# Tokens sorted by expert on TensorE and moved to the expert pages in runs by SP, in place of row scatters by GpSimd, in a fused GNN and mixture-of-experts kernel

## The chip, the core and the metric

One core of a Trainium2 chip. The metric is the device time of one execution in microseconds. The kernel before took 3548.45 us, the median of three runs (3544.21 to 3556.92).

## What is computed

A graph layer over 12,500 nodes and 212,500 weighted edges, then a mixture of eight experts, each token going to its best expert only and each expert taking at most C = 1,954 tokens, in order of the token's number. Cut to what matters:

```python
# graph layer: features of the source nodes, weighted, summed by destination
msgs = features[edge_src] * edge_weight[:, None]
agg = jax.ops.segment_sum(msgs, edge_dst, num_segments=12500)
gnn = agg @ W.T + b                                  # features = layernorm(x)
x = x + gnn
# experts: h = layernorm(x)
logits = h @ gate_w + gate_b
idx = argmax(softmax(logits))                        # one expert for each token
pos = cumsum(one_hot(idx))[token, idx] - 1           # place in that expert's list
kept = pos < C
buf[idx, pos] = h                                    # for the kept tokens
y = (relu(buf @ w1 + b1) @ w2 + b2)[idx, pos] * prob * kept
x = x + nan_to_num(y)
```

All data are float32; x has 256 columns, an expert 1,024 hidden ones. With the reference's inputs the experts get between 781 and 3,325 tokens, and no expert gets more than 46 of the 128 tokens of one tile.

## The kernel before

**Edges.** Edges come sorted by destination. They are cut in 1,661 edge tiles of 128. For each, GpSimd (POOL) gathers 128 rows of the normalized features by an indirect DMA (`gather`, L582), VectorE (DVE) builds a 128x128 matrix of edge weights by destination (`onehot`, L590), and TensorE (PE) multiplies the two (`product`, L599), summing 15 edge tiles in PSUM. ScalarE (ACT) copies such a group sum out (L602). The gathered tiles `m` have 32 buffers.

**Nodes.** A generator, `nodes`, works through 98 tiles of 128 nodes in chunks of eight tiles (the last chunks have 5, 4 and 1). For each node tile it shifts and adds the group sums (L635), multiplies with W (L644), adds x (L647). `Ffn.route` then normalizes the chunk, computes the gate and the best expert of each token, and its place in the expert's list (`pre`, `pos`), and makes rows `rt` of 260 columns: the token's 256 values, mean, inverse deviation, probability and number.

**Pages.** `buf` in HBM holds 128 pages of 128 rows, 16 for each expert, filled at the start with a value that names no token. `put` (L341) scatters the 128 rows of one node tile to their places in the pages, by an indirect DMA of POOL. Each is queued in `pool_q` and issued one per step. `listing` then finds which pages have become full, and `nodes` waits until the queue is empty before it hands these pages to the experts.

**Experts.** A second generator, `experts`, loads a page or a pair of pages (`load`, L439) and the expert's weights (1 MB each for w1 and w2) by SP, 20 steps before it uses them; `fresh` normalizes (L459), `turn` transposes, `products` multiplies (L483 and L494), `finish` scales, and `send` (L525) scatters the finished rows to the output by an indirect DMA of POOL. Chunks 0 to 9 hand over pairs, chunks 10 to 12 single pages, and after the last chunk all full pages left and each expert's last, partly filled page follow.

**The order.** One loop writes all of this out by hand. Each step of it issues one gather, then one scatter from `pool_q` or else a piece of a finished page's work, then the products of the edge tile that was gathered 16 steps earlier (`LEAD`), then one yield of `nodes` and one of `experts`. Pieces of expert work are spaced by `PACE` (3.0 steps for pairs, 2.3 for single pages). Every engine works its queue in this order. After step 1,661 there are no gathers left and the loop goes on until the pages are done.

Each DMA signals one of eight semaphores of its kind in turn: eight for the DMAs of POOL, eight that SP and ACT share. A DMA waits for the one that had its semaphore before.

**Two guards.** `rest` works off more single pages when the lists were longer than planned, and a slow path recomputes everything when `n_bad`, a count of edges out of the expected order, is not zero.

Of the kernel before, what the change touches and what calls it, by code (L numbers as in the profile page):

```python
# [9 lines left out]
F32 = mybir.dt.float32  # L10
# [8 lines left out]
P = 128  # L19
# [26 lines left out]
FILL = float(1 << 20)  # L46


SLOTS = [(2, n) for n in (0, 3, 4, 4, 4, 4, 4, 4, 4, 2)] + [(1, n) for n in (10, 4, 3)]
# [9 lines left out]
LOADED = 20  # L59
PACE = {1: 2.3, 2: 3.0}  # L60


# [32 lines left out]
def gnn_moe_kernel(ctx: ExitStack, tc: tile.TileContext, x, src, dst, ew, wT, gb, gate_w, gate_b,  # L95
# [6 lines left out]
    feat = dram.tile([N, D], F32, name="feat")  # L102
    buf = dram.tile([(NP_ + 2) * P, RW], F32, name="buf")

    ident = consts.tile([P, P], F32, name="ident")
# [43 lines left out]
    nc.vector.tensor_scalar(need, even, float(P), float(P), op0=ALU.mult, op1=ALU.add)  # L149
    n_bad = consts.tile([1, 1], I32, name="n_bad")  # L150

    gb_sb = consts.tile([P, D], F32, name="gb_sb")
# [4 lines left out]
    keep = ctx.enter_context(tc.tile_pool(name="keep", bufs=1))  # L157
    run = keep.tile([P, E], F32, name="run")
    posted = keep.tile([P, 1], F32, name="posted")
    place_of = keep.tile([P, 1], F32, name="place_of")  # L160
# [58 lines left out]
    class Ffn:  # L219
        def __init__(self, p3, p4, ps_m, ps_t, ps_h, ps_y):  # L220
            self.p3, self.p4 = p3, p4
            self.ps_m, self.ps_t, self.ps_h, self.ps_y = ps_m, ps_t, ps_h, ps_y
            self.puts, self.sends, self.loads = [], [], []
            self.paired = False

            self.before = None
# [4 lines left out]
            nc.vector.memset(taken, 0.0)  # L231

        def fill(self):
# [11 lines left out]

        def route(self, rt, ln, t0, nt, rows):
            p3 = self.p3
# [91 lines left out]

            def put(j):  # L340
                s = nc.gpsimd.indirect_dma_start(  # L341
                    out=buf[:, :], out_offset=bass.IndirectOffsetOnAxis(ap=to[:, j, :], axis=0),
                    in_=rt[:rows, j, :], in_offset=None, bounds_check=NP_ * P - 1, oob_is_err=False)
# [6 lines left out]
                self.before = s  # L350

            self.put = [(put, j) for j in range(nt)]


# [57 lines left out]
        def last(self):  # L412
            p3 = self.p3
            c8 = p3.tile([P, E], F32, name="c8")
            nc.vector.tensor_mul(c8, run, mine)
            c = p3.tile([P, 1], F32, name="c1")
            nc.vector.tensor_reduce(c, c8, axis=AX.X, op=ALU.add)
            nc.vector.tensor_scalar(c, c, float(C), page0, op0=ALU.min, op1=ALU.subtract)
            some = p3.tile([P, 1], F32, name="some")
            nc.vector.tensor_scalar(some, c, 1.0, None, op0=ALU.is_ge)  # L420
            nc.vector.scalar_tensor_tensor(some, c, float(P), some, op0=ALU.is_lt, op1=ALU.mult)
            nc.vector.tensor_scalar(c8, mine, some, None, op0=ALU.mult)
            pi = self.psum("pi")
            nc.tensor.matmul(pi[0:1, :E], page_of[:, 0:1], c8, start=True, stop=True)
            lp = p3.tile([1, E], I32, name="lp", bufs=1)
            nc.vector.tensor_scalar(lp, pi[0:1, :E], float(NP_ * P), None, op0=ALU.add)
            return lp

        def load(self, of, li, i, e=None):
            p4 = self.p4  # L430
            at = li[0:1, 0, i:i + 1] if e is None else li[0:1, e:e + 1]
# [6 lines left out]
            pg = p4.tile([P, 2, RW], F32, name="pg", bufs=4)  # L438
            self.loads.append(nc.sync.dma_start(  # L439
                pg[:, :of, :], buf[ds(row, of * P), :].rearrange("(a p) d -> p a d", p=P)))  # L440
            return (of, pg) + self.weights(e)
# [58 lines left out]
        def finish(self, of, pg, py, b2_sb):  # L500
# [22 lines left out]

            def send(a):
                s = nc.gpsimd.indirect_dma_start(  # L525
                    out=out[:, :], out_offset=bass.IndirectOffsetOnAxis(ap=to[:, a, :], axis=0),
                    in_=z[:, a, :], in_offset=None, bounds_check=N - 1, oob_is_err=False)
                for o in self.sends:
                    if o is not self.before:
                        tc.declare_no_dep(s.ins, o.ins, reason="each token is in one page")  # L530
                self.sends.append(s)
                self.before = s

# [12 lines left out]
        def rest(self):  # L546
            left = nc.values_load(left_i, min_val=0, max_val=LEFT,  # L547
                                  skip_runtime_bounds_check_because="a count of pages")
            with tc.If(left > 0):
                self.sends, self.before = [], None  # L550
                for i in range(4):
                    self.page(1, self.li, i)
                with tc.If(left > 4):
                    self.sends = []
                    for i in range(4, LEFT):
                        self.page(1, self.li, i)


    with tc.tile_pool(name="edges", bufs=1) as edges:
# [8 lines left out]
        with tc.tile_pool(name="p2", bufs=32) as p2, tc.tile_pool(name="p2h", bufs=12) as p2h, \  # L568
# [8 lines left out]
            sums, ms, hs = {}, {}, {}  # L577
            pool_q, pages = [], []

            def gather(k):  # L580
# [3 lines left out]
                    in_offset=bass.IndirectOffsetOnAxis(ap=src_i[:, k:k + 1], axis=0))  # L584
                ffn.before = None
                ms[k] = m
# [18 lines left out]
            def nodes():  # L605
# [10 lines left out]
                for c, (t0, nt, rows) in enumerate(CHUNKS):  # L616
                    rt = p3.tile([P, CH, RW], F32, name="rt")
                    ln = ln_new(p3)
                    for t in range(t0, t0 + nt):
# [32 lines left out]
                    last = c == len(CHUNKS) - 1  # L652
                    if last or SLOTS[c][1]:
# [68 lines left out]
            def check():  # L722
# [17 lines left out]
                nc.tensor.matmul(pc, ones[:, 0:1], cnt, start=True, stop=True)  # L740
                nc.vector.tensor_scalar(n_bad, pc, -1.0, float(P * KT), op0=ALU.mult, op1=ALU.add)

# [106 lines left out]
            for f, j in pool_q:  # L849
# [4 lines left out]

    some = nc.values_load(n_bad[0:1, 0:1], min_val=0, max_val=P * KT,
                          skip_runtime_bounds_check_because="a count of edges")
    with tc.If(some > 0):
# [132 lines left out]
```

## Time and profile before

| | |
|---|---|
| median of three runs | 3548.45 us |
| the profiled execution | 2575.36 us |
| its span, first to last instruction | 2573.6 us |
| mean granted TensorE clock in it | 0.867 |
| indirect DMAs of POOL: gathers, scatters to pages, scatters to the output | 1661, 98, 91 |
| mean time of one: gather from the features, to pages, to the output | 972, 1009, 1001 ns |

The profiled execution is shorter than the runs by some 973 us; the profile shows that execution only. PE, DVE, ACT, POOL and SP are the engines' names in it, PEld is the loading of a matmul's stationary operand, and a q behind an engine's name means its queue or sequencer. In the lines of groups the number after x counts instructions; a float32 product counts as two matmul instructions. The slices show the course of the run:

```profile
PE   2467788797799698698699699698698797698797
PEld 1345545575577477477487487477476574487686
DVE  6775433444344344354453444444443443454432
ACT  5750000111012012012012012012011110122232
POOL 7647777777777777777777777777777777777111
PEclk9678666799799799799799799799799797799898
```

Each digit is the busy share in tenths of a fortieth of the span, 64 us; PEclk is the granted clock in tenths. The first three slices are the normalizing of the features, the last three come after the last gather. Between them a chunk of eight node tiles repeats about every 190 us.

### The profile page before, as it was taken

The numbers are of one execution on the slowest core, as the hardware profiler recorded it, in microseconds if no ns is written. First come the engines' busy times: TensorE is split into PE (matmuls) and PEld (weight loads), VectorE is DVE, ScalarE is ACT, GpSimd is POOL, SyncE is SP. The second block draws the span as 40 slices with busy tenths as digits, with TensorE's granted clock in tenths as the row PEclk, the third lists the DMA queues.
The fourth block names the chain that finished last, engine by engine and source line by source line (L and its number), as shares of the span: only waits on it lengthen the run. The fifth ranks groups of instructions, "written<-read, shape, count | busy, mean of one in ns | idle before, by whom it ended". The sixth has DMA issues, their size and how long they took to land. (4 is left out here: it accounts for less than half of the span.)

```text
span 2573.6 us, 30236 instructions
## 1 busy us (share of the span) xinstructions
PE 2046.4 (80%) x9082; PEld 1599.7 (62%) x9082; DVE 1177.0 (46%) x4287; ACT 504.9 (20%) x1315; POOL 1805.4 (70%) x1859
## 2 busy tenths in 40 slices
PE   2467788797799698698699699698698797698797
PEld 1345545575577477477487487477476574487686
DVE  6775433444344344354453444444443443454432
ACT  5750000111012012012012012012011110122232
POOL 7647777777777777777777777777777777777111
PEclk9678666799799799799799799799799797799898
DMA  8759434644654654654654654654654354497485
GB/s 282 252 172 368 127 109 124 193 145 122 211 166 123 219 157 122 209 165 121 204 170 122 201 175 122 204 170 123 194 177 121 110 186 122 138 309 247 153 273 176
DMA packets 264700, 455.60 MB, mean 177 GB/s; under 512 B 44799, under 2 KB 190406, under 8 KB 264520
## 3 DMA queue, kind: packets, MB, share of 16 engines
q0 software_dynamic: 88800, 240.41, 30.5%
q1 hardware_dynamic: 136210, 174.68, 21.1%
q10 hardware_dynamic: 39510, 38.41, 4.6%
q8 instruction: 77, 1.26, 0.2%
q14 instruction: 103, 0.84, 0.1%
HBM read 387.86 MB, written 67.83 MB: 177 GB/s over the span
## 5 line engine op out<-in xcount | busy, mean ns | idle before, releaser
L582 POOL DMA_INDIRECT m<-feat,src_i x1549 | 1506.2, 972 | 493.0 <-issue 222.1
L599 PE MATMUL pw<-m,h 128*128 128x256 f32 x3322 | 1114.9, 451 | 408.7 <-DMA m<-feat,src_i 297.8
L599 PEld LDWEIGHTS pw<-m,h 128*128 128x128 f32 x3322 | 654.0, 219 | 701.9 <-DMA m<-feat,src_i 406.2
L590 DVE TENSOR_SCALAR h<-cols,rel,w_sb 128x128 f32<-128x128 f32 x1549 | 467.0, 360 | 405.6 <-PE pw L599 397.3
L483 PE MATMUL ph<-gT,w_sb 128*128 128x256 f32 (+1 forms) x1856 | 362.7, 346 | 0.0
L494 PE MATMUL py<-w_sb,hT 128*128 128x256 f32 x1456 | 349.8, 385 | 0.0
L483 PEld LDWEIGHTS ph<-gT,w_sb 128*128 128x128 f32 x1856 | 308.7, 199 | 33.3
L494 PEld LDWEIGHTS py<-w_sb,hT 128*128 128x128 f32 x1456 | 274.6, 193 | 35.1
L487 ACT ACTIVATE hT<-ph,b_sb 128x256 f32<-128x256 f32 (+1 forms) x464 | 167.9, 426 | 419.4 <-PE ph L483 409.7
L525 POOL DMA_INDIRECT out<-z,tok x91 | 91.1, 1001 | 153.2 <-DVE tok L522 111.7
L635 PEld LDWEIGHTS ms<-s,ws 128*128 128x128 f32 x1116 | 177.1, 216 | 18.2 <-issue 3.7
L635 PE MATMUL ms<-s,ws 128*128 128x128 f32 x1116 | 176.3, 299 | 3.4 <-DVE s L612 3.3
L647 DVE TENSOR_TENSOR rt<-xt,ms 128x256 f32<-128x256 f32 x98 | 41.2, 420 | 287.8 <-PE ms L644 287.7
L602 ACT COPY ws<-pw 128x256 f32<-128x256 f32 x111 | 41.4, 373 | 631.6 <-PE pw L599 631.6
L582 POOL DMA_INDIRECT m<-in_x,src_i x112 | 108.1, 965 | 53.6 <-issue 20.1
L504 DVE TENSOR_TENSOR y<-py,b_sb 128x512 f32<-128x512 f32 (+1 forms) x58 | 33.4, 576 | 240.4 <-PE py L494 240.4
L341 POOL DMA_INDIRECT buf<-rt,to x98 | 98.9, 1009 | 54.0 <-issue 19.2
L459 DVE TENSOR_SCALAR xg<-pg 128x256 f32<-128x256 f32 x91 | 35.3, 418 | 174.1 <-DMA pg<-buf 174.1
L507 ACT ACTIVATE y<-y,pg 128x256 f32<-128x256 f32 x91 | 42.6, 502 | 340.4 <-DVE y L504 294.5
L644 PE MATMUL ms<-wT_sb,aT 128*128 128x256 f32 x392 | 107.4, 399 | 2.4 <-ACT aT L639 2.4
L639 ACT COPY aT<-ms 128x256 f32<-128x256 f32 x98 | 36.5, 373 | 275.6 <-PE ms L635 269.9
L644 PEld LDWEIGHTS ms<-wT_sb,aT 128*128 128x128 f32 x392 | 77.4, 199 | 15.8 <-ACT aT L639 4.4
(159 smaller groups left out, 1253.6 us busy)
## 6 DMA issues: line engine op xcount, KB each, us to landing
w_sb<-in_w SPq DMA_DIRECT2D x116, 1024.0 KB, 11.4
m<-feat,src_i POOLq DMA_INDIRECT x1549, 2.8
buf<-fill SPq DMA_DIRECT2D x13, 1300.0 KB, 18.4
xt<-in_x ACTq DMA_DIRECT2D x97, 128.0 KB, 2.4
xt<-in_x SPq DMA_DIRECT2D x12, 1024.0 KB, 8.1
feat<-xn ACTq DMA_DIRECT2D x12, 1024.0 KB, 9.7
out<-rt ACTq DMA_DIRECT2D x11, 1024.0 KB, 4.9
pg<-buf SPq DMA_DIRECT2D x33, 260.0 KB, 13.4
```

Of the source, the lines that this page charges most:

```text
L341: s = nc.gpsimd.indirect_dma_start(out=buf[:, :], out_offset=bass.IndirectOffsetOnAxis(ap=to[:, j, :], axis=0), in_=rt[:rows, j, :], in_of ...
L483: nc.tensor.matmul(ph[:, c:c + n], w1_sb[:, k, f * P:(f + 1) * P], xT[:, k * n:(k + 1) * n], start=(k == 0), stop=(k == 1))
L487: nc.scalar.activation(hT[:, f, :n], ph[:, c:c + n], AF.Relu, bias=b1_sb[:, f:f + 1])
L494: nc.tensor.matmul(py[:, a, :], hT[:, f, a * P:(a + 1) * P], w2_sb[:, f, :], start=(f == 0), stop=(f == F // P - 1))
L507: nc.scalar.activation(y[:, a, :], y[:, a, :], AF.Copy, scale=pg[:, a, D + 2:D + 3])
L525: s = nc.gpsimd.indirect_dma_start(out=out[:, :], out_offset=bass.IndirectOffsetOnAxis(ap=to[:, a, :], axis=0), in_=z[:, a, :], in_offset= ...
L582: nc.gpsimd.indirect_dma_start(out=m, out_offset=None, in_=x[:, :] if k < RAW else feat[:, :], in_offset=bass.IndirectOffsetOnAxis(ap=src_ ...
L590: nc.vector.tensor_scalar(h, cols, rel[:, k:k + 1], w_sb[:, k:k + 1] if w is None else w, op0=ALU.is_equal, op1=ALU.mult)
L599: nc.tensor.matmul(product.pw, hs.pop(k), ms.pop(k), start=(j == 0), stop=last)
L602: nc.scalar.copy(ws, product.pw)
L635: nc.tensor.matmul(pa[:, k * P:(k + 1) * P], sums[g][:, k * P:(k + 1) * P], shifts[t, g], start=(g == gs[0]), stop=(g == gs[-1]))
L644: nc.tensor.matmul(px[:rows, :], aT[:, k * P:k * P + rows], wT_sb[:, k, :], start=(k == 0), stop=(k == 1))
```

## The change

- The node tiles of chunks 0 to 10 (`SORTED = 11`, eleven chunks of eight tiles) are no longer scattered row by row. `sort` builds for each tile a 128x128 permutation from the tokens' places within the tile, ordered by expert (L590's kind of operation), multiplies `rt` with it on TensorE, copies the sorted rows back over `rt`, and stores the chunk into one of three HBM tensors, `by_expert`, from ACT's queue.
- For each tile and expert, `move` copies 64 rows (`RUN`) from the place where the expert's run begins in `by_expert` to the expert's next free row in the pages, HBM to HBM, by SP. Both row numbers are loaded into registers from SBUF, four at a time. A run is shorter than 64 rows as a rule; the rows behind it are overwritten by the expert's next run, which therefore waits for the move of the same expert before it. Two moves are issued per step of the loop (`MOVES`), from a queue of their own, and `nodes` waits until both queues are empty.
- Where an expert's last run leaves foreign rows behind the last token of a page, `fresh` adds a large number to their token number when the partly filled pages are worked off (`none`, `part`).
- If an expert has more than 64 tokens in a tile (`most`), the slow path is taken.
- Scatters of POOL (`put` of chunks 11 to 13, and `send`) no longer wait for the one before; a `nop` stands ahead of each.

```diff
+RUN = 64
+MOVES = 2
+SORTED = 11
...
+    by_expert = [dram.tile([CH * P + RUN, RW], F32, name=f"by_expert{i}") for i in range(3)]
...
         def fill(self):
...
+            for s in by_expert:
+                nc.sync.dma_start(s[CH * P:, :], fill[:RUN, :])
...
             pre = small("pre")
+            if place is not None:
+
+                runs = p3.tile([P, CH, 2, E], I32, name="runs")
+                off = p3.tile([P, CH, E], F32, name="off")
+                nc.vector.memset(off[:, :, 0:1], 0.0)
+                for e in range(E - 1):
+                    nc.vector.tensor_add(off[:, :nt, e + 1], off[:, :nt, e], pp[:, 1, :nt, e])
+                nc.vector.tensor_add(pre, pp[:rows, 0, :nt, :], off[:rows, :nt, :])
+                nc.vector.tensor_add(runs[0:1, :nt, 0, :], off[0:1, :nt, :],
+                                     tokc[0:1, :nt, None].to_broadcast([1, nt, E]))
...
             for j in range(nt):
-                nc.vector.tensor_add(pre[:, j, :], pp[:rows, 0, j, :], run[:rows, :])
+                if place is None:
+                    nc.vector.tensor_add(pre[:, j, :], pp[:rows, 0, j, :], run[:rows, :])
+                else:
+                    nc.vector.scalar_tensor_tensor(runs[0:1, j, 1, :], run[0:1, :], float(C), pages_of,
+                                                   op0=ALU.min, op1=ALU.add)
                 nc.vector.tensor_add(run, run, pp[:, 1, j, :])
...
+            if place is not None:
+                nc.vector.tensor_scalar_add(pos, pos, -1.0)
+                yield from self.sort(rt, pos, runs, place, nt, rows)
+                return
...
             def put(j):
+                nc.gpsimd.nop()
                 s = nc.gpsimd.indirect_dma_start(
...
                 for i in self.puts:
-                    if i is not self.before:
-                        tc.declare_no_dep(s.ins, i.ins, reason="each token has a row of its own")
+                    tc.declare_no_dep(s.ins, i.ins, reason="each token has a row of its own")
...
+        def sort(self, rt, pos, runs, place, nt, rows):
+            for j in range(nt):
+                r = self.p3.tile([P, P], F32, name="perm")
+                nc.vector.tensor_scalar(r[:rows, :], cols[:rows, :], pos[:, j, :], None,
+                                        op0=ALU.is_equal)
+                yield
+                ps = self.psum("ps")[:, :RW]
+                nc.tensor.matmul(ps, r[:rows, :], rt[:rows, j, :], start=True, stop=True)
+                nc.scalar.copy(rt[:, j, :], ps)
+            yield
+            nc.scalar.dma_start(place[:nt * P, :].rearrange("(j p) d -> p j d", p=P), rt[:, :nt, :])
+
+            at = {}
+
+            def move(j, e):
+
+                nc.sync.nop()
+                for i, f in ((0, e), (1, e)) if e % 4 == 0 else ():
+                    _, v = nc.values_load_multi_w_load_instructions(
+                        runs[0:1, j, i, f:f + 4], engines=[mybir.EngineType.SP], min_val=0,
+                        max_val=((E - 1) * PE_ * P + C if i else CH * P),
+                        skip_runtime_bounds_check_because="rows of the chunk, and of the pages")
+                    at.update(((i, f + a), v[a]) for a in range(4))
+                s = nc.sync.dma_start(buf[ds(at[1, e], RUN), :], place[ds(at[0, e], RUN), :])
+                for i in self.moves:
+                    if i is not self.moved[e]:
+                        tc.declare_no_dep(s.ins, i.ins, reason="another expert's, or one before that")
+                for i in self.loads:
+                    tc.declare_no_dep(s.ins, i.ins, reason="pages that are read are full")
+                self.moves.append(s)
+                self.moved[e] = s
+
+            self.put = [(move, j, e) for j in range(nt) for e in range(E)]
...
         def fresh(self, of, pg):
             xg = self.p4.tile([P, 2, D], F32, name="xg")
+            if self.part[id(pg)] is not None:
+                nc.vector.tensor_add(pg[:, 0, D + 3:RW], pg[:, 0, D + 3:RW], self.part[id(pg)])
...
             def send(a):
+                nc.gpsimd.nop()
...
-                    yield from ffn.route(rt, ln, t0, nt, rows)
-                    pool_q.extend(ffn.put)
+                    yield from ffn.route(rt, ln, t0, nt, rows,
+                                         by_expert[c % 3] if c < SORTED else None)
+                    (moves if c < SORTED else pool_q).extend(ffn.put)
...
-                        while pool_q:
+                        while moves or pool_q:
                             yield
...
                 if s < KT:
                     gather(s)
+                for f, j, e in moves[:MOVES]:
+                    f(j, e)
+                del moves[:MOVES]
                 if pool_q:
                     f, j = pool_q.pop(0)
                     f(j)
```

More of the change, by code (lines that the diff above doesn't have):

```diff
@@ L150, in gnn_moe_kernel @@
     n_bad = consts.tile([1, 1], I32, name="n_bad")
+    bad = consts.tile([1, 1], F32, name="bad")
+    pages_of = consts.tile([1, E], F32, name="pages_of")
+    nc.vector.tensor_scalar(pages_of, cols[0:1, :E], float(PE_ * P), None, op0=ALU.mult)
     gb_sb = consts.tile([P, D], F32, name="gb_sb")
@@ L158, in gnn_moe_kernel @@
     run = keep.tile([P, E], F32, name="run")
+    most = keep.tile([1, 1], F32, name="most")
     posted = keep.tile([P, 1], F32, name="posted")
@@ L223, in __init__ @@
             self.puts, self.sends, self.loads = [], [], []
+            self.part = {}
             self.paired = False
-            self.before = None
             nc.vector.memset(run, 0.0)
@@ L231, in __init__ @@
             nc.vector.memset(taken, 0.0)
+            nc.vector.memset(most, 0.0)
+            self.moved, self.moves = [None] * E, []
         def fill(self):
@@ L243, in psum, with route @@
             return self.ps_m.tile([P, 512], F32, name="ms")
-        def route(self, rt, ln, t0, nt, rows):
+        def route(self, rt, ln, t0, nt, rows, place=None):
             p3 = self.p3
@@ L319, in route @@
             pre = small("pre")
-            for j in range(nt):
-                nc.vector.tensor_add(pre[:, j, :], pp[:rows, 0, j, :], run[:rows, :])
+            if place is not None:
[7 more added lines that the diff above has]
+                                     tokc[0:1, :nt, None].to_broadcast([1, nt, E]))
+                much = p3.tile([1, 1], F32, name="much")
+                nc.vector.tensor_reduce(much, pp[0:1, 1, :nt, :], axis=AX.XY, op=ALU.max)
+                nc.vector.tensor_tensor(most, most, much, op=ALU.max)
+            for j in range(nt):
+                if place is None:
[3 more added lines that the diff above has]
+                                                   op0=ALU.min, op1=ALU.add)
                 nc.vector.tensor_add(run, run, pp[:, 1, j, :])
@@ L349, in put @@
                 self.puts.append(s)
-                self.before = s
             self.put = [(put, j) for j in range(nt)]
+        def sort(self, rt, pos, runs, place, nt, rows):
[27 more added lines that the diff above has]
+            self.put = [(move, j, e) for j in range(nt) for e in range(E)]
         def split(self):
@@ L426, in last @@
             nc.vector.tensor_scalar(lp, pi[0:1, :E], float(NP_ * P), None, op0=ALU.add)
+            cs = p3.tile([P, E], F32, name="cs", bufs=1)
+            nc.vector.tensor_scalar(cs, c8, c, None, op0=ALU.mult)
+            pc = self.psum("pc")[:, :E]
+            nc.tensor.matmul(pc, ones, cs, start=True, stop=True)
+            self.none = p3.tile([P, E], F32, name="none", bufs=1)
+            nc.vector.tensor_scalar(self.none, pc, pcol, float(SKIP), op0=ALU.is_le, op1=ALU.mult)
             return lp
@@ L430, in load @@
             p4 = self.p4
+            none = None if e is None else self.none[:, e:e + 1]
             at = li[0:1, 0, i:i + 1] if e is None else li[0:1, e:e + 1]
@@ L438, in load @@
             pg = p4.tile([P, 2, RW], F32, name="pg", bufs=4)
+            self.part[id(pg)] = none
             self.loads.append(nc.sync.dma_start(
@@ L528, in send @@
                 for o in self.sends:
-                    if o is not self.before:
-                        tc.declare_no_dep(s.ins, o.ins, reason="each token is in one page")
+                    tc.declare_no_dep(s.ins, o.ins, reason="each token is in one page")
                 self.sends.append(s)
-                self.before = s
             for _ in range(3):
@@ L549, in rest @@
             with tc.If(left > 0):
-                self.sends, self.before = [], None
+                self.sends = []
                 for i in range(4):
@@ L577, in gnn_moe_kernel @@
             sums, ms, hs = {}, {}, {}
-            pool_q, pages = [], []
+            moves, pool_q, pages = [], [], []
             def gather(k):
@@ L584, in gather @@
                     in_offset=bass.IndirectOffsetOnAxis(ap=src_i[:, k:k + 1], axis=0))
-                ffn.before = None
                 ms[k] = m
@@ L649, in nodes @@
                         ln_stats(ln, x1, t - t0, rows)
-                    yield from ffn.route(rt, ln, t0, nt, rows)
-                    pool_q.extend(ffn.put)
+                    yield from ffn.route(rt, ln, t0, nt, rows,
+                                         by_expert[c % 3] if c < SORTED else None)
+                    (moves if c < SORTED else pool_q).extend(ffn.put)
                     last = c == len(CHUNKS) - 1
+                    if last:
+                        nc.vector.scalar_tensor_tensor(n_bad, most, float(RUN), bad, op0=ALU.is_gt,
+                                                       op1=ALU.add)
                     if last or SLOTS[c][1]:
@@ L740, in check @@
                 nc.tensor.matmul(pc, ones[:, 0:1], cnt, start=True, stop=True)
-                nc.vector.tensor_scalar(n_bad, pc, -1.0, float(P * KT), op0=ALU.mult, op1=ALU.add)
+                nc.vector.tensor_scalar(bad, pc, -1.0, float(P * KT), op0=ALU.mult, op1=ALU.add)
             B = CH + RB
@@ L851, in gnn_moe_kernel @@
             ffn.rest()
-    some = nc.values_load(n_bad[0:1, 0:1], min_val=0, max_val=P * KT,
-                          skip_runtime_bounds_check_because="a count of edges")
+    some = nc.values_load(n_bad[0:1, 0:1], min_val=0, max_val=P * KT + 1,
+                          skip_runtime_bounds_check_because="a count of edges, and one")
     with tc.If(some > 0):
```

## The prediction

> **What bounds the kernel now.** I read the engines' totals and slices first, then the table of stretches, then the groups, then Pool's order of time.
>
> ```profile
> span 2573.6 us, 30236 instructions
> PE 2046.4 (80%) x9082; PEld 1599.7 (62%) x9082; DVE 1177.0 (46%) x4287; ACT 504.9 (20%) x1315; POOL 1805.4 (70%) x1859
> ```
>
> PE is the busiest by share, Pool second. The stretches turn this round:
>
> ```profile
> 1400.00:1600.00 200.00, 169.05 (x770) 136.94 (x768) 88.69 (x313) 33.43 (x78) 152.26 (x157) 0.90 0.53 164
> 1600.00:1800.00 200.00, 165.92 (x765) 132.55 (x765) 90.61 (x316) 33.75 (x77) 152.20 (x157) 0.93 0.53 163
> ...
> 2400.00:2500.00 100.00, 82.84 (x508) 75.01 (x507) 40.49 (x178) 33.60 (x101) 13.63 (x14) 0.88 0.66 209
> ```
>
> Columns: stretch, length, busy us of PE, PEld, DVE, ACT, POOL (instructions), granted TensorE clock, DMA share, GB/s. From 400 to 2200 us Pool issues 155 to 159 operations in every 200 us, whatever PE does. That is a rate limit; its two parts stand in Pool's timeline:
>
> ```profile
> 2217.69 0.94 POOL L582 DMA_INDIRECT m<-feat,src_i  x1 [0.30 <-PE ms L635]
> 2218.93 1.00 POOL L341 DMA_INDIRECT buf<-rt,to  x1 [0.30 <-issue]
> 2220.24 0.98 POOL L582 DMA_INDIRECT m<-feat,src_i  x1 [0.30 <-PE ms L635]
> 2221.53 1.02 POOL L341 DMA_INDIRECT buf<-rt,to  x1 [0.30 <-issue]
> ```
>
> The bracket is always 0.30 us, whoever is named as releaser: it is the sequencer's own gap. A gather costs 1.25 us, a scatter to the pages (L341) 1.31. PE's waits point the same way:
>
> ```profile
> L599 PE MATMUL pw<-m,h 128*128 128x256 f32 x3322 | 1114.9, 451 | 408.7 <-DMA m<-feat,src_i 297.8
> ...
> L341 POOL DMA_INDIRECT buf<-rt,to x98 | 98.9, 1009 | 54.0 <-issue 19.2
> ```
>
> PE waits for gathered rows. So Pool carries this execution until its last gather at about 2380 us; then PE works off expert pages, one per 7.59 us (2468.80 to 2476.38 here; x is the number of matmuls):
>
> ```profile
> 2468.80 3.62 PE L494 MATMUL py<-w_sb,hT 128*128 128x256 f32 x16
> 2472.25 3.73 PE L483 MATMUL ph<-gT,w_sb 128*128 128x128 f32 x32
> 2476.14 0.41 PE L468 MATMUL pT<-ident,xg 128*128 128x128 f32 x2
> 2476.38 3.62 PE L494 MATMUL py<-w_sb,hT 128*128 128x256 f32 x16
> ```
>
> One thing doesn't fit: the profiled execution took 2575.4 us (span 2573.6 and 1.8 around it), the median of the runs is 3548.45. No view names the missing 973 us. One resource of the trace has two speeds:
>
> ```profile
> 924.10:927.60 3.50, 3.50 (x9) 2.75 (x9) 0.36 (x1) 0.00 (x0) 2.59 (x4) 0.50 0.70 225
> ```
>
> ```profile
> 924.23 3.62 PE L483 MATMUL ph<-gT,w_sb 128*128 128x256 f32 x8
> ```
>
> At clock 0.50 eight 256-column matmuls take 3.62 us; at 1.00 sixteen do (above).
>
> **What the Trainium skill says.** "DMA: Bandwidth & Descriptors", section Issuing engines are not separate DMA queues: SP, ACT and Pool feed the same 16 engines, and another issuer saves only issue time. Here issue time is what binds, and the engines have room (share 0.53), so the advice is met. The same page, Two DMAs through the same engine are not ordered: only a completion semaphore orders them; hence an expert's runs, which overlap, wait for one another. No run here has such copies. The same page, Anatomy of one DMA: 2.0 us plus bytes at 436 GB/s; the old scatters land after 2.6 us, which agrees. "TensorE: Matmul & The Clock Gate", Part 1: the clock is at half or full, and work releases it; the 0.50 and 1.00 above agree.
>
> **The change part by part.**
>
> Removed: 88 of 98 scatters (chunks 0 to 10; 5 + 4 + 1 stay). Each 1.009 busy and 0.30 gap: 88 x 1.31 = 115 us of Pool, on the path. Pool's instruction order has nothing in their place, and its nops leave no instruction. Waits between scatters were 11.7 us in all for L341, nearly all after the last gather, where the chain of the last chunks runs beside waiting pages: counted at nothing.
>
> Added on PE: per tile a sort of 128x260, two matmuls at 0.22 us (clock 1.00) to 0.44 (0.50): 39 to 77 us in all. Cover: PE idles 31 to 34 us in each 200 us above, and a chunk of eight tiles needs 3.5 to 7. Nothing on the path; uncovered, it costs the whole 77.
>
> Added on DVE and ACT: 88 permutations like L590 (0.36 us) 32 us; 88 copies of a PSUM tile like L602 (0.373) 33 us; some 25 short operations per chunk at about 0.1 us, 28 us. DVE is busy 45%, ACT 17%: nothing.
>
> Added on ACT's queue: one 1 MB store per chunk, like the store of out rows already there (4.9 us to landing). It is issued after the sort, and the moves wait for it.
>
> Added on SP: 704 moves of 64 rows (66 KB, HBM to HBM) with 352 register loads. SP's issues stand 0.60 us apart and a pair of register loads adds 0.67:
>
> ```profile
> 1064.66 0.35 SPq L446 DMA_DIRECT2D b_sb<-in_b  x1
> 1065.26 0.34 SPq L448 DMA_DIRECT2D b_sb<-in_b  x1
> 1065.84 0.38 SPq L450 DMA_DIRECT2D w_sb<-in_w  x1
> 1066.45 0.38 SPq L452 DMA_DIRECT2D w_sb<-in_w  x1
> 1067.72 0.37 SPq L439 DMA_DIRECT2D pg<-buf  x1
> ```
>
> A tile is 8 x 0.60 + 2 x 0.67 = 6.1 us, a chunk 49. A move's own time is unseen. Below: 2.15 us, an estimate by the page's formula; above: 8.8 us, the median landing of a 130 KB page load behind weights. An expert's next move is eight later, so it can hold SP at 8.8 / 8 = 1.1 us a move at worst, 70 us a chunk. I take 49. Queued behind the moves on SP are the page load L439 and the weights; DVE waits for these (174 us in 21 waits already) and PE behind it. Cover: Pool may run 16 gathers (20 us) further before the 32 buffers of m stop it. The moves start about 13 steps ahead of Pool, because ACT runs that far ahead of it, and are written over 32 steps = 40 us: 49 us end within 3 us of the place where the loads stand. Nothing at 49; at 70 about the cushion.
>
> Moved: counting the yields, the sort takes 9 steps more and the moves 32 where eight scatters took 8: each listing gets its pages 33 steps later. In the middle chunks pages fill 116 of 135 steps and only shift. At the end they don't: chunk 10's pages start 33 steps later, a page takes 12 steps, so 33 / 12 = 2.75 pages more are left after the last gather, at 7.59 us: +21 us.
>
> Sum: -115 + 21 = **-94 us**, so 2481 for the profiled execution. Carried to the runs: 3548 - 94 = 3454 if the missing 973 us are a fixed piece; 3548 x (1 - 94/2575) = 3418 if everything is slower there. Nothing separates the two; I take the middle, **3436**. Own range 3400 to 3490.
>
> **The rivals.**
>
> (a) *TensorE is the bound in the runs; slower.* Mechanism: the runs are granted a clock near 0.50. All matmuls at 0.50: 6230 of 256 columns at 0.432 (16 in 3.45 us, doubled) = 2691; 2292 of 128 at 0.24 = 550; some 560 short ones at up to 0.24 = 134; with 114 us of PE idle in the first 200 us: 3489, within 2% of 3548. For it: this fit. Against: in this trace dense work releases the clock within a few us, and a PE that is always busy should not stay at half. It decides where 1688 / clock + 114 passes the 2573 that Pool needs, below a clock of 0.69. Then freeing Pool gives nothing, and the 88 sorts cost 88 x 2 x 0.439 = 77: **3625**.
>
> (b) *Moves come late; slower.* From 79 us a chunk (1.24 us a move) the delay past the 20 us cushion, 10 us in each of nine chunks, eats the 94. At 1.5 us a move: 96 - 49 - 20 = 27 us, nine times, less 94: +149, **about 3700**. Against it: SP otherwise mostly waits for lists.
>
> (c) *The freed time is only partly used*, because PE, with less idle time and bursts of pages at full load, holds the buffers of m: half to all of it lost, **3500 to 3548**.
>
> That the change leaves its path, through a run over 64 rows, I rule out: the reference's inputs have at most 46 tokens of an expert in a tile.
>
> **How the numbers follow.** Forecast 0.44, (a) 0.38, (b) 0.08, (c) 0.10. A run of this kernel can tell 0.3% (11 us) from no change: (c) gives 0.04 faster and 0.06 same; faster 0.48, same 0.06, slower 0.46. The range reaches from the forecast's lower end over (a): 3400 to 3640; what is left out is (b) and tails, under 2 in 10. The forecast's own range is above.
>
> **What would show it.** Pool's L341 group at 10; Pool 155 to 160 operations in 200 us still, now nearly all gathers; last gather near 2265; moves about 0.75 us apart on SP; a tail of some 215 us after the last gather. Wrong if PE in the middle stretches is over 95% busy, if Pool's gathers wait for PE by more than 0.3 us each, or if the profiled execution gets some 94 us faster and the runs don't: that is (a).

## The result, and the profile after

| | before | changed |
|---|---|---|
| median of the runs | 3549.89 us (4 runs, 3544.21 to 3556.92) | 3676.26 us (4 runs, 3663.18 to 3679.73) |
| ratio, 95% interval | | 1.0348 (1.0316 to 1.038): slower |

The forecast was 3436 us, in a range of 3400 to 3640. The change costs 126 us where 112 were to be gained.

The kernel before takes some 2570 us on some chips and some 3550 us on others, as the first experiment shows. Its profiled execution came from the first kind, called A from here on; every time of the table above, and the profile after, came from the second, called B. A page of B set beside a page of A therefore shows the chip and the change together. From the page of the changed kernel:

```profile
PE 2068.3 (56%) x9260; PEld 1703.6 (47%) x9260; DVE 1187.4 (32%) x4487; ACT 533.6 (15%) x1403; POOL 1692.6 (46%) x1771
...
L664 POOL DMA_INDIRECT m<-feat,src_i x1549 | 1481.6, 957 | 1061.4 <-PE pw L680 451.4
...
L609 POOL DMA_INDIRECT out<-z,tok x91 | 92.2, 1013 | 796.6 <-DVE tok L605 547.3
...
L551 PE MATMUL pT<-ident,xg 128*128 128x128 f32 x182 | 39.4, 336 | 307.2 <-DVE xg L542 302.2
...
L542 DVE TENSOR_SCALAR xg<-pg 128x256 f32<-128x256 f32 x91 | 35.2, 418 | 360.1 <-DMA pg<-buf 360.1
```

No engine is the bound here: the busiest, PE, works 56% of the span of 3661.4 us. POOL has its 88 operations fewer (1771 against 1859) and a gather still takes 957 ns, but the idle time ahead of the gathers has doubled, from 493 to 1061 us. Three waits stand out: VectorE's scaling of a page's rows (`xg`) waits 360 us for page loads, TensorE's first product on it (`pT`) waits 302 us for VectorE, and POOL's scatters to the output wait 547 us for their token numbers. How much of this is the chip, the comparison with A cannot tell. The 547 us are no sign of late pages by themselves: the one kernel without moves that was profiled on B, the kernel before with doubled products (below), has 574 us of that wait, and no wait of `xg` for page loads among its waits. A stretch of the middle (columns as before) shows the fall of POOL's rate from 157 operations in 200 us to 97:

```profile
1400.00:1600.00 200.00, 99.91 (x421) 81.56 (x421) 53.02 (x205) 18.61 (x44) 90.98 (x97) 0.73 0.44 132
```

### The profile page after: what moved, and what is told of

It reads as the page before. It is cut to its first block, busy times and chain, and to the rows that moved or that the text cites. A ratio compares the mean times of both kernels' runs of the same rounds, so it can differ in the third digit from the quotient of the medians.

```text
span 3661.4 us, 33997 instructions
## 1 busy us (share of the span) xinstructions
PE 2068.3 (56%) x9260; PEld 1703.6 (47%) x9260; DVE 1187.4 (32%) x4487; ACT 533.6 (15%) x1403; POOL 1692.6 (46%) x1771
## 5 line engine op out<-in xcount | busy, mean ns | idle before, releaser
L664 POOL DMA_INDIRECT m<-feat,src_i x1549 | 1481.6, 957 | 1061.4 <-PE pw L680 451.4
L680 PE MATMUL pw<-m,h 128*128 128x256 f32 x3322 | 995.3, 428 | 320.8 <-issue 172.5
L680 PEld LDWEIGHTS pw<-m,h 128*128 128x128 f32 x3322 | 693.6, 218 | 460.8 <-issue 210.2
L577 PE MATMUL py<-w_sb,hT 128*128 128x256 f32 x1456 | 408.1, 419 | 138.2 <-issue 133.2
L577 PEld LDWEIGHTS py<-w_sb,hT 128*128 128x128 f32 x1456 | 302.9, 212 | 201.9 <-issue 159.0
L725 PE MATMUL ms<-wT_sb,aT 128*128 128x256 f32 x392 | 128.2, 457 | 377.6 <-ACT aT L720 206.0
L551 PE MATMUL pT<-ident,xg 128*128 128x128 f32 x182 | 39.4, 336 | 307.2 <-DVE xg L542 302.2
L295 PE MATMUL ms<-gw_sb,xT 128*128 128x8 f32 x392 | 69.8, 287 | 206.6 <-ACT xT L290 115.0
L295 PEld LDWEIGHTS ms<-gw_sb,xT 128*128 128x128 f32 x392 | 65.9, 235 | 242.2 <-ACT xT L290 145.1
L551 PEld LDWEIGHTS pT<-ident,xg 128*128 128x128 f32 x182 | 26.4, 173 | 318.3 <-DVE xg L542 303.6
```

The costliest lines, as they stand in the source:

```text
L295: nc.tensor.matmul(pl[:rows, :], xT[:, k, :rows], gw_sb[:, k, :], start=(k == 0), stop=(k == 1))
L551: nc.tensor.transpose(pt[:, k * n + a * P:k * n + (a + 1) * P], xg[:, a, k * P:(k + 1) * P], ident)
L577: nc.tensor.matmul(py[:, a, :], hT[:, f, a * P:(a + 1) * P], w2_sb[:, f, :], start=(f == 0), stop=(f == F // P - 1))
L664: nc.gpsimd.indirect_dma_start(out=m, out_offset=None, in_=x[:, :] if k < RAW else feat[:, :], in_offset=bass.IndirectOffsetOnAxis(ap=src_ ...
L680: nc.tensor.matmul(product.pw, hs.pop(k), ms.pop(k), start=(j == 0), stop=last)
L725: nc.tensor.matmul(px[:rows, :], aT[:, k * P:k * P + rows], wT_sb[:, k, :], start=(k == 0), stop=(k == 1))
```

## The experiments

Runs whose names begin with c or e ran on one chip beside the kernel before, so did those of d, f, g and h each; only the group of f came to a chip of kind B. Ratios are to the kernel before of the same group.

| run | chip | median us | ratio, 95% interval |
|---|---|---|---|
| c0_before_again | A | 2571.26 | 1.0006 (0.9997 to 1.0015) |
| e1_unsorted | A | 2580.97 | 1.0041 (1.0025 to 1.0057) |
| e2_before_plus_products | A | 2573.24 | 1.0012 (1.0003 to 1.0021) |
| e3_pages_later | A | 2576.31 | 1.0019 (1.001 to 1.0028) |
| d1_after_again | A | 2610.62 | 1.0137 (1.0115 to 1.0158) |
| d2_after_later | A | 2548.36 | 0.99 (0.9883 to 0.9916) |
| d3_short_moves | A | 2607.22 | 1.0134 (1.0117 to 1.0151) |
| d4_unsorted_later | A | 2531.66 | 0.984 (0.9819 to 0.986) |
| f1_sorted_9_later | B | 3488.86 | 0.9826 (0.9802 to 0.985) |
| f2_before_double | B | 3710.51 | 1.046 (1.0432 to 1.0487) |
| f3_after_double | B | 3770.11 | 1.0621 (1.0596 to 1.0646) |
| f4_unsorted_double | B | 3694.45 | 1.0406 (1.0377 to 1.0436) |
| g1_unsorted_again | A | 2583.76 | 1.0042 (1.0025 to 1.0059) |
| g2_later_again | A | 2547.55 | 0.9914 (0.9888 to 0.994) |
| g3_products_again | A | 2575.28 | 1.0008 (0.9998 to 1.0017) |
| g4_sorted_9_again | A | 2506.63 | 0.9749 (0.9727 to 0.9771) |
| h1_sorted_9 | A | 2579.30 | 1.0039 (1.0024 to 1.0054) |
| h2_unsorted_9_later | A | 2495.05 | 0.9719 (0.9691 to 0.9748) |

### The parts of the change one by one

**The kernel before, once more.** No edit.

> The kernel before, run once more for a profile of it as the timed runs have it. Theory A (in the runs TensorE is held back: it works at full speed for 25 to 45 us, then nearly stops for 20 to 30 us, as in the profile after the change): ratio 1.00, and the profile is now about 3550 us long, PE's busy share 55 to 60%, granted clock near 0.76, with some 30 stretches in which only a few matmuls start in 10 us. Theory B (the missing 973 us lie outside the span or come from Pool): the profile is again about 2575 us, or Pool's gathers take 1.7 us or more each.

Its runs took what its profiled execution had taken, 2571 us. So the 973 us that no view named are no piece of the program, and nothing that timing adds to profiling: they come with the chip on which it runs. No record shows one and the same chip in both kinds. (The theories A and B in the expectations of this group are guesses at the cause, not the two kinds of chip.)

**Unsorted**: stores, moves and order of the changed kernel, without permutation, product and copy.

```diff
-                r = self.p3.tile([P, P], F32, name="perm")
-                nc.vector.tensor_scalar(r[:rows, :], cols[:rows, :], pos[:, j, :], None,
-                                        op0=ALU.is_equal)
                 yield
-                ps = self.psum("ps")[:, :RW]
-                nc.tensor.matmul(ps, r[:rows, :], rt[:rows, j, :], start=True, stop=True)
-                nc.scalar.copy(rt[:, j, :], ps)
```

> The changed kernel without the sort itself: no permutation, no product on TensorE, no copy back (the rows go to the pages unsorted, so the pages hold wrong tokens); stores, moves, register loads and the order in time stay. Theory A: the 88 products of 260 columns are 2 to 3% of TensorE's work, so the time falls from 3676 by 80 to 130 us, to 3545 to 3600. Theory B (the moves, their SP queue or the DMA traffic cost the time): it stays within 20 us of 3676.

2581 us: POOL's 88 scatters are gone, TensorE has no sort, and still 11 us are lost. Something other than the sort eats 115 us of POOL.

**The products alone**: the kernel before with 88 products of the sort's size.

```diff
+            rs = []
+            if nt == CH and rows == P:
+                for j in range(nt):
+                    r = p3.tile([P, P], F32, name="perm", bufs=8)
+                    nc.vector.tensor_scalar(r, cols, pos[:, j, :], None, op0=ALU.is_equal)
+                    rs.append(r)
...
+                if rs:
+                    ps = self.psum("ps")[:, :RW]
+                    nc.tensor.matmul(ps, rs[j], rt[:, j, :], start=True, stop=True)
```

> The kernel before with 88 products of the sort's size added beside its scatters (the permutation is built from another column and the result is not used); no moves, no store, no delay. Theory A: +70 to +130 us, 3620 to 3680. Theory B: within 15 us of 3549, since Pool or transfers bind and TensorE has room.

+3 us: on a chip of kind A they are hidden.

**The delay alone**: the kernel before, its first eleven lists of pages 33 steps later.

```diff
                         while pool_q:
                             yield
+                        for _ in range(33 if c < 11 else 0):
+                            yield
```

> The kernel before with nothing changed but that each of the first eleven lists of pages is handed over 33 steps later, as in the changed kernel. If the late pages cost what the prediction says: +21 us. Theory A: TensorE's work is only shifted and it is the bound to the end: 0 to +15 us. A rival (late pages are the main cost of the change): +60 us or more.

+6 us (1.0019), where the prediction's step had 21. The products and the delay are cheap by themselves, and without the sort a loss remains, so the next place to look is what is left, the moves and what waits for them.

### Where the moves' time goes

**The changed kernel on A.** No edit.

> The changed kernel itself, beside the kernel before on one chip. Theory L (late pages: the moves of a chunk take 74 to 88 us on SP instead of the 32 turns of the loop, some 40 us, that the program's order gives them; the page loads behind them are late, VectorE stands at the page, the token numbers and so the scatter to the output are late, and Pool gives its 115 us back): on a chip where before takes 2570 us it lies just above the unsorted version, 2580 to 2600 (ratio 1.004 to 1.012). Theory T (the whole loss is TensorE's, which that other chip held back): the same there, since this chip does not hold it back, and again 1.035 only where before takes 3550 us. Theory S (the loss of 3.5% belongs to the program on every chip): about 2660.

2611 us, +39 and 1.4%: a loss here as well, but not that of B. It lies 11 us above the range of theory L and far from that of S. Who waits about the page tile `pg` (us, times; first who held `xg` up, then who waited for the readers of `pg`):

```profile
  DMA pg<-buf: 385.4, 20
...
  DVE xg L542: 385.4, 20
...
  PE pT L551: 275.2, 19
  POOL out L609: 247.6, 28
```

The same of the kernel before, on A:

```profile
  DVE xg L459: 174.1, 21
  POOL out L525: 111.7, 16
...
  PE pT L468: 9.4, 8
```

One chunk in order of time shows how one wait makes the next. SP moves the last runs and then issues the page load (start, us, instruction):

```profile
1316.11 8.13 SPq L415 DMA_DIRECT2D buf<-by_expert  x9
1326.77 0.40 SPq L520 DMA_DIRECT2D pg<-buf  x1
```

VectorE had come to this page at 1306.4, and stood there with all its later work:

```profile
1306.18 0.18 DVE L191 BATCH_NORM_AGGREGATE mv<-bn 128x2 f32<-128x6 f32 x1
1330.38 0.88 DVE L542 TENSOR_SCALAR xg<-pg 128x256 f32<-128x256 f32 x2 [24.02 <-DMA pg<-buf]
```

TensorE stood as long:

```profile
1331.00 1.22 PE L551 MATMUL pT<-ident,xg 128*128 128x128 f32 x4 [23.90 <-DVE xg L542]
```

POOL gathered on until 1363.5, when the next scatter to the output came up in its order:

```profile
1362.51 0.95 POOL L664 DMA_INDIRECT m<-feat,src_i  x1 [0.30 <-issue]
1374.01 1.00 POOL L609 DMA_INDIRECT out<-z,tok  x1 [10.54 <-DVE tok L605]
```

The scatter needs the output rows and token numbers of that page, for which VectorE and TensorE stood 24 us; the scatter, and the gathers behind it, wait 10.5 us. In the trace's order of gathers each of the chunks 1 to 10 has one such place, where 11 to 28 us lie from one gather to the next, 160 us together; less the 2.6 that a scatter between two gathers takes anyway these are 134 us, more than the 115 saved. Up to the last gather the scatters to the output waited 155 us in all, against 22 in the kernel before; the waits of the gathers themselves hardly changed (561 against 546, the 0.30 us before each included).

**Later lists**: the page work stands in the program's order 30 steps later.

```diff
                         while moves or pool_q:
                             yield
+                        for _ in range(30 if c < SORTED else 0):
+                            yield
```

> The changed kernel with each of the first eleven lists of pages handed over 30 turns of the loop later, so that the page work stands in the program's order where its data is really there. Theory L: VectorE's wait for pg (360 us in the unsorted version) falls under 100, the waits of the scatters to the output for tok fall to the 112 us of before, and the time falls by most of Pool's saving: 2490 to 2530 where before takes 2570 (ratio 0.97 to 0.985). Theory T: later pages only push work to the end, as they did before (+6 us): 2585 to 2610 there. Where before takes 3550 us, L says a gain of 50 us or more against the changed kernel, T says none.

2548 us, 62 less than the changed kernel and 1% less than the kernel before; a repeat gave 2547.55. The waits about `pg` fell, VectorE's below the 100 us expected, those of the scatters to the output only to 170 where 112 were expected:

```profile
  DMA pg<-buf: 91.9, 8
...
  POOL out L609: 170.4, 23
  DVE xg L542: 91.9, 8
  PE pT L551: 63.5, 16
```

POOL is back at its rate, first the changed kernel, then this one, both on A:

```profile
1400.00:1600.00 200.00, 161.23 (x779) 135.43 (x777) 97.51 (x350) 36.97 (x89) 145.36 (x151) 0.91 0.62 190
```

```profile
1400.00:1600.00 200.00, 176.51 (x795) 143.99 (x795) 95.28 (x330) 38.24 (x91) 151.94 (x158) 0.91 0.64 196
```

Theory L's cause holds on A, and theory T, with 2585 to 2610, does not; L's size does not hold either: 2490 to 2530 was expected. The last gather starts at 2276 us (2374 before), so 98 us are won by then; 272 us lie behind it instead of 198, so 74 are given back.

**Short moves.**

```diff
-                s = nc.sync.dma_start(buf[ds(at[1, e], RUN), :], place[ds(at[0, e], RUN), :])
+                s = nc.sync.dma_start(buf[ds(at[1, e], 16), :], place[ds(at[0, e], 16), :])
```

> The changed kernel with moves of 16 rows instead of 64 (of a run longer than 16 rows the rest isn't moved, so pages lack these rows; 16.6 KB a move instead of 66.6). It has the same instructions and waits, a quarter of the moves' data. If the moves are long because their data lands late (each waits for the one before of its expert, and they share the DMA engines with the gathers and weights), a chunk's moves shorten from 74 to 88 us to 50 to 55, the pages come some 25 us sooner, and the time falls to 2500 to 2550 where before takes 2570. If issuing and the start of the moves set it: within 10 us of the changed kernel.

2607 us, like the changed kernel. The moves of a middle chunk took 63 to 67 us, against 64 to 67. A quarter of the data changes nothing: what takes the time is issuing the moves, not their bytes.

**Unsorted, with later lists.** Both edits together.

> As the run with the lists 30 turns later, but without the permutation, its product and its copy back (rows go to the pages in their old order, so tokens land in wrong experts' pages). Beside that run it gives the price of the sort alone: 0 to 10 us where TensorE is not held back (88 products of about 0.45 us, beside others), and 40 to 80 us where it is (theory T: 77 us at half the clock).

2532 us, 17 less than with the sort, where 0 to 10 were expected. Without later lists the sort costs more: the changed kernel's 2611 stand against 2581 and 2584 of the two runs of the unsorted version, 27 to 30 us, though not on one chip. With later lists the last gather of the unsorted version starts at 2259, 115 us before that of the kernel before, which is POOL's whole saving.

### A better split

**Nine sorted chunks, later lists**: also `SORTED = 9`. It ran on B first.

> The changed kernel with the lists 30 turns later, and only nine chunks sorted instead of eleven: chunks 9 and 10 are scattered by Pool as before, their lists not delayed. With eleven sorted and later lists the last gather came 98 us before that of the kernel before (2276 against 2374), but 272 us lay behind it instead of 198. If that growth is page work that the late lists push past the gathers: 16 scatters come back on Pool (+21 us at 1.31), the last gather stands near 2297, the end 200 to 215 behind it, so 2495 to 2515 where before takes 2570 (ratio 0.97 to 0.98). If the tail is long for another reason (page work that TensorE must do anyway), it stays near 270: 2565.

> Nine chunks sorted, their lists 30 turns later, once more. Where before takes 2570 us: 2495 to 2515 if the long tail was page work pushed past the gathers, 2565 if it was not. Where before takes 3550 us it repeats 3489.

On A 2507 us, inside the expected 2495 to 2515: the last gather at 2307, 196 us behind it. So the long tail goes when the last two chunks are left to POOL with lists that are not late. The edit changes both at once: eleven sorted chunks with only the first nine lists late were not run. The tails of the two versions, from 2276 with eleven chunks and from 2300 with nine:

```profile
2276.00:2548.00 272.00, 225.35 (x1436) 203.31 (x1436) 107.76 (x438) 87.43 (x268) 35.13 (x37) 0.93 0.69 225
```

```profile
2300.00:2504.00 204.00, 157.04 (x1014) 142.41 (x1012) 73.30 (x297) 64.03 (x196) 29.98 (x31) 0.90 0.63 205
```

TensorE works at over 75% in both; with eleven it has 68 us more to do there (225.35 - 157.04).

On B it took 3489 us, 63 less than the kernel before and 187 less than the changed kernel had taken in the first measurement. There, too, the waits about `pg` are smaller than in the changed kernel, whose 360 and 547 us stand above:

```profile
  POOL out L609: 293.4, 28
...
  DVE xg L542: 42.3, 4
```

This version beats both kernels on both kinds of chip.

**Its two neighbours**: nine chunks without later lists, and with later lists but unsorted.

> The changed kernel with nine chunks sorted and lists handed over as it does, not later. Beside the nine-chunk version with later lists it gives the price of the late pages alone. Where before takes 2570 us that price is 9/11 of the 62 us it was with eleven: 2550 to 2565 (ratio 0.992 to 0.998). Where before takes 3550 us the later version took 3489: theory T (the sort's TensorE work is the whole loss there) puts this one at 3480 to 3510 too; theory L (late pages lose time there as well) at 3540 to 3620.

> The nine-chunk version with later lists, without the permutation, its product and its copy (tokens land in wrong experts' pages). It gives the price of the sort of 72 tiles alone. Where before takes 2570 us: 2485 to 2500 (9/11 of 17 us under 2507). Where before takes 3550 us: theory T says 60 us or more under 3489, theory L under 20.

2579 us without later lists, more than the 2550 to 2565 expected: lateness costs 73 us here. It is 31 us less than with eleven sorted chunks, so leaving two chunks to POOL pays without later lists as well. 2495 us unsorted: the sort of 72 tiles costs 12.

### Chips of kind B

**Each gather's product twice**, in the kernel before, in the changed kernel, and in the unsorted one.

```diff
-                nc.tensor.matmul(product.pw, hs.pop(k), ms.pop(k), start=(j == 0), stop=last)
+                nc.tensor.matmul(product.pw, hs[k], ms[k], start=(j == 0), stop=False)
+                nc.tensor.matmul(product.pw, hs.pop(k), ms.pop(k), start=False, stop=last)
...
-                    nc.scalar.copy(ws, product.pw)
+                    nc.scalar.activation(ws, product.pw, AF.Copy, scale=0.5)
```

> The kernel before with each product of a gather made twice into the same sum, which is halved on its copy back: the same result, with 1661 products more on TensorE (some 750 us by the rows of the page), and nothing else. It makes TensorE the bound on a chip that doesn't hold it back, as a stand-in for the chip that does. Expected 2850 to 3200 where before takes 2570; under 2700 TensorE would still not be the bound and the stand-in fails.

> The changed kernel with each product of a gather made twice, as in the doubled kernel before. Theory T (where TensorE is the bound the sort's products are the loss, and Pool's saving is worth nothing): 40 to 80 us over the doubled before, ratio 1.015 to 1.03. Theory L (late pages lose it): with TensorE the bound, the steps of the loop are longer, the moves are on time and pages no longer late, so the doubled kernels differ by under 20 us. Both together (TensorE stands still at late pages and can't make it up): over 80 us.

> The unsorted version (changed kernel without the permutation, its product and its copy, so tokens land in wrong experts' pages) with each product of a gather made twice. Theory T: equal to the doubled before within 15 us, the whole loss being the sort. If late pages cost TensorE-bound time: 30 us or more over the doubled before without any sort.

They were meant for A, as a stand-in for B, and came to B itself. There 1661 more products, 731 us of TensorE by 0.22 us a matmul, cost the kernel before 159 us:

```profile
PE 2670.7 (72%) x12404; PEld 2277.4 (61%) x12404; DVE 1172.8 (32%) x4287; ACT 503.3 (14%) x1315; POOL 1783.3 (48%) x1859
```

So TensorE was not full on B either. Of the doubled kernels the changed one is 60 us over before, and the unsorted one 16 under it. That is what theory T forecast for a kernel bound by TensorE (40 to 80 us over, and the same within 15 without the sort). The sort costs 76 us in this company; the same two versions, undoubled, differ by 27 to 30 us on A. How much of the 76 comes from B and how much from the doubling can't be told, since no doubled kernel ran on A.

**Three repeats**, which would have told more on B, came to A; they confirm the first readings there.

> The changed kernel without the permutation, its product and its copy (tokens land in wrong experts' pages), once more. Where before takes 3550 us, theory T (the loss is the sort's TensorE work) says 3530 to 3560, some 110 to 130 us under the changed kernel's 3676; theory L (late pages) says 3630 to 3660, since the pages are as late without the sort. Where before takes 2570 us it repeats 2581.

> The changed kernel with eleven lists 30 turns later, once more. Where before takes 3550 us, theory T says 3650 to 3690, as the changed kernel, since it has the same TensorE work; theory L says under 3600. Both parts: between. Where before takes 2570 us it repeats 2548.

> The kernel before with 88 products of the sort's size beside its scatters, once more. Where before takes 3550 us, theory T says 40 to 120 us more than before (ratio 1.011 to 1.034); if the sort's cost lies in its place in the chain of a chunk and not in its TensorE work, under 20 us. Where before takes 2570 us it repeats +3.

## Why the prediction was wrong

- **POOL bounds it, and 88 scatters are worth 115 us: right on A.** Unsorted with later lists, the last gather comes 115 us sooner. On B the nine-chunk version gains 63 us, so POOL's time has worth there too.
- **The step that failed, as the runs on A show it: "Nothing at 49; at 70 about the cushion".** Two terms of it were wrong. The first is 0.60 us a move, read from issues 0.35 to 0.38 us long. A move's issue is longer, as this line of the changed kernel on A has it (ns, min/median/max):

```profile
L415 SPq DMA_DIRECT2D buf<-by_expert x704: 520/521/1337, 291.6 to 2317.4; - x176
```

  Moves stand 0.77 us apart, eight with their register loads take 7.6 us where nothing holds them, so a chunk takes 61 us, not 49; with waits the middle chunks took 64 to 67 on A and the first three and last two 76 to 116. The second term is the cushion of 20 us. Buffers of `m` for 16 more gathers say how long POOL can go on without TensorE, and POOL did go on. But VectorE and TensorE had no cushion, and stood 21 to 24 us in each middle chunk; and POOL's own queue holds scatters to the output, which need their work. In the chunk shown VectorE stood 24.0 us and POOL 10.5, so the cushion was some 13.5 us. An estimate from these figures: moves of 49 us instead of the 65.6 measured there would have left VectorE some 7 us and POOL none, so "nothing at 49" agrees with the trace, and the size of the moves and the cushion together made the loss. The prediction asked who waits for the page loads, and stopped at TensorE.
- **Sorts hidden, VectorE and ScalarE free: nearly.** 88 products beside other work cost 3 us on A, the sort in its place 17 with later lists (12 for 72 tiles) and 27 to 30 without. Why more, was not tried; the store and the moves wait for it.
- **+21 us for late pages: three pages more are left after the last gather, as counted** (22 scatters to the output against 19), but the tail grew by 10 us, from 198 to 208.
- **Carrying it to the runs.** The prediction took the missing 973 us for a fixed piece or a factor. They come with the kind of chip, and so does the size of the loss: 39 us on A, 126 on B. No step of the prediction had such a dependence.
- **Rival (a), TensorE the bound at half clock**, gave 3625, the closest number, but its mechanism does not hold, so much of that is luck. It needs a granted clock below 0.69, and the changed kernel's runs on B had 0.76 to 0.77, with TensorE busy 56%. Its 77 us for the sorts are near the 76 of the doubled kernels; that freeing POOL gives nothing is what fails. Were TensorE the bound at half clock, 1661 more products at 0.44 us a matmul would have cost 1462 us, not 159, and 72 sorts with POOL's saving worth nothing could not have come out 63 us faster.
- **Rival (b), late moves**, had the mechanism, as far as A goes, and set its point at 79 us a chunk. 65 are enough, because the loss goes through VectorE and POOL's queue rather than through the buffers of `m`. When a move's data lands is in no trace, so its 2.15 us, worked out by a formula for DMAs of POOL, stay unchecked; the short moves show that the bytes do not set the pace.

What stays open: how the 126 us on B divide. The waits for page loads are there, and they fall with the nine-chunk version, but no run takes the lateness alone away. The unsorted version and the one with eleven later lists never ran there undoubled. The doubled kernels put 76 us on the sort; the 187 us between the changed kernel and the nine-chunk version hold the lateness, 16 sorts and the shorter tail, not separated.

## What to carry to other kernels

When work moves to an idle queue, follow its result to the last consumer, and look in each consumer's queue for what stands behind the waiting instruction: here a load late on SP stopped VectorE, and through a scatter in POOL's own order the gathers that had been freed. Price a new DMA by its own form, not by its neighbours' issues. And where a program's order is written out by hand, an added delay has to be written into that order too: on A 30 empty steps turned a loss of 1.4% into a gain of 1%, and leaving the last two chunks alone made it 2.5%.

## What the hardware showed unasked

The same kernel takes 2570 us on chips of kind A and 3550 on kind B. On B TensorE runs for some tens of us and then nearly stops with nothing that the profile shows to wait for. The changed kernel's PE, then its POOL in the same stretch:

```profile
1749.18 1.03 PE L577 MATMUL py<-w_sb,hT 128*128 128x256 f32 x4
...
1752.72 0.38 PE L577 MATMUL py<-w_sb,hT 128*128 128x256 f32 x1 [1.75 <-issue]
1755.63 0.58 PE L577 MATMUL py<-w_sb,hT 128*128 128x256 f32 x1 [2.53 <-issue]
```

```profile
1752.05 0.94 POOL L664 DMA_INDIRECT m<-feat,src_i  x1 [0.30 <-issue]
1753.30 0.95 POOL L664 DMA_INDIRECT m<-feat,src_i  x1 [0.30 <-issue]
```

The Trainium skill, "TensorE: Matmul & The Clock Gate", Part 1, explains a halved clock by TensorE's own idleness. The trace agrees that the clock is low where TensorE stands: 0.58 from 1750 to 1769 us, 0.90 in the 22 us behind. That is not all of it here, since SP is slow in the same stretch: ten moves took 29 us on B, and twenty took 19 us on A.

```profile
1745.42 29.07 SPq L415 DMA_DIRECT2D buf<-by_expert  x10
```

```profile
1271.56 18.79 SPq L415 DMA_DIRECT2D buf<-by_expert  x20
```

Even a register move on SP is stretched. Its line for the moves on A, then on B (ns, min/median/max):

```profile
L415 SPq MOVE buf<-by_expert x1408: 29/29/38, 291.5 to 2317.3; - x176
```

```profile
L415 SPq MOVE buf<-by_expert x1408: 2/29/1587, 365.1 to 3340.1; - x176
```

Within the stops of 1750 to 1769 and 1791 to 1829 us (TensorE works for some 7 us of the second), SP's register moves have a median of 0.70 us instead of 0.029, while POOL's gathers keep 0.95. So in these stretches the instruction streams of PE and SP are slowed together, and POOL's is not. The change gives SP 3175 instructions more (4475 against 1300 in the traces), and a chunk's moves took 102 to 152 us on B. That this makes the loss there is not shown: in the nine-chunk version, which gains 63 us, SP has 3905 instructions and a chunk's moves took 113 to 155 us. What slows the two streams was not found.
